# Expert layer as seven products of block sums for two token tiles

## The chip, the cores and the metric

The kernel runs on one core of one Trainium2 chip. Its engines are TensorE (PE, with its weight loads listed apart as PEld), VectorE (DVE), ScalarE (ACT), GpSimd (POOL) and SyncE (SP), which here issues the DMAs. They run side by side and wait for each other through semaphores. The metric is the time of the program on the device in microseconds; the kernel before takes 1626.39 us, the median of 3 runs (1625.09 to 1628.73).

## The reference

Four layers are applied to 1024 tokens of width 512 (16 x 64), each an attention and a feed-forward part added to the stream. The part that is changed is the third feed-forward, a layer of 64 experts of rank 16, in which every token takes its best 16 experts:

```
scores = xf @ Wr.T
top_vals, top_idx = jax.lax.top_k(scores, TOPK)
gates = jax.nn.softmax(top_vals, axis=-1)
G = jnp.zeros((N, K), xf.dtype).at[jnp.arange(N)[:, None], top_idx].set(gates)
h = jnp.einsum('nd,krd->nkr', xf, A)
out = jnp.einsum('nkr,kdr->nd', h * G[:, :, None], B)
return (out * SCALING).reshape(*prefix, -1)
```

All experts are computed for all tokens: a dense product of (tokens x 512) by (512 x 1024), a multiplication by the gates (zero for the experts not taken), and a product by (1024 x 512). Everything is in 32-bit floating point.

## The kernel before, in words

The tokens are 8 tiles of 128. Two lanes share the core, each with four of the eight PSUM banks and its own pools in SBUF: lane a allocates from the left, lane b from the right. Each lane is written as a generator that yields a cost in microseconds after each piece of work. `merged` runs lane a as the main one, and after each yield advances lane b by pieces whose costs add up to the same (times a rate). PE's order is this written order. The order of the other engines and of SP's queue is chosen by the framework's planner from the dependences and its own costs; each queue is then run in order.

Lane b does the first layer, then the second feed-forward (`mxfp4_ffn`) and the last layers for the first four tiles; lane a does the second layer's attention (`normed_attention`) for all eight tiles, then the same rest for the last four tiles. So lane b's `mxfp4_ffn` (about 750 to 850 us) and most of its expert layer (1039 to 1134 us) lie beside lane a's attention, the end of the latter beside lane a's `mxfp4_ffn`, and lane a's expert layer (1291 to 1412 us) lies beside lane b's last attention, `packed_attention`. From about 1450 us lane a is alone.

`mxfp4_ffn` quantises four tiles of weights (lane b only) and four of tokens by long chains of DVE instructions (L979 to L1004), turns them on PE (ps_mx) and multiplies. `small_head_attention` precedes the expert layer in each lane; its weights take three of the lane's pages, which are four buffers of 128 x 2048 f32 used in turn.

`lora_experts` loads four pages of weights (L1242), normalises and transposes the lane's tiles (`Normed`), and then runs four steps over the tiles, one behind the other: `router` (scores, the best 16, the gates), `hidden` (two PSUM banks of 512 columns, four products each, L1290, then a DVE multiplication by the gates, L1298), `turn` (eight transposes and two ACT copies, L1308) and, a tile later, `output` (eight products of 512 columns in one bank, L1315, and one DVE addition to the stream, L1318). A 128x512 f32 product appears in the trace as two records of PE. `packed_attention` follows; it starts by normalising the lane's first tiles and multiplying by the value weights (ps_v, L1411).

Of the kernel before, what the change touches and what calls it, by code (L numbers as in the profile page):

```python
# [8 lines left out]
F32 = mybir.dt.float32  # L9
F16 = mybir.dt.float16  # L10
F32R = mybir.dt.float32r
BF16 = mybir.dt.bfloat16
# [6 lines left out]
P = 128  # L19
# [27 lines left out]

PAGE = 2048


# [1000 lines left out]

def small_head_attention(ln, tiles, w_in):

# [14 lines left out]
    with ExitStack() as es:  # L1068
# [141 lines left out]

        for n in range(NTL + 3):
            if 0 <= n - 2 < NTL:
                values(n - 2)
                yield 1.0
# [15 lines left out]

def lora_experts(ln, tiles, w_a, w_r, w_b):


    k, nc = ln.k, ln.nc
    KE, R = 64, 16
    KR = KE * R
    SCALING = 2.0
    wa, wb = [], []
    for ws, src in ((wa, w_a), (wb, w_b)):
        for i in range(2):  # L1240
            ws.append(ln.page("w_l2f", PAGE))
            nc.sync.dma_start(ws[i], src[:, i * PAGE : (i + 1) * PAGE])  # L1242
    wa = [w[:, c * KR : (c + 1) * KR] for w in wa for c in range(2)]
    wb = [w[:, j * D : (j + 1) * D] for w in wb for j in range(4)]
    with ExitStack() as es:
        pool = ln.pool(es, "l2f")
        wr = w_r.rearrange("p (c n) -> p c n", c=NC)
        normed = Normed(ln, pool, tiles)
        normed.begin()
        yield 2.5  # L1250
        normed.need(-1)
        kept = {}

        def router(t):
            normed.need(tiles.index(t))
            ps = ln.bank([P, KE], "ps_r")
# [9 lines left out]
            for i in range(2):  # L1266
# [5 lines left out]
                best.append(m8)  # L1272
            gate = pool.tile([P, KE], F32, tag="gate", name="gate")
            nc.vector.tensor_tensor(gate, left, sc, ALU.not_equal)
# [6 lines left out]
            nc.vector.tensor_scalar_mul(gate, gate, sm[:, 1:2])  # L1281
            kept[t] = gate

        def hidden(t):
            gate = kept[t]
            hg = pool.tile([P, KE, R], F32, tag="hg", name="hg")
            for i in range(2):
                ps = ln.bank([P, KE // 2, R], "ps_h")
                for c in range(NC):
                    nc.tensor.matmul(  # L1290
                        ps,
                        lhsT=k.stream(c, t),
                        rhs=wa[c][:, i * 512 : (i + 1) * 512],
                        start=c == 0,
                        stop=c == NC - 1,
                    )
                part = slice(i * KE // 2, (i + 1) * KE // 2)
                nc.vector.tensor_tensor(  # L1298
                    hg[:, part, :], ps, bc(gate[:, part], 2, R), ALU.mult
                )  # L1300
            kept[t] = hg

        def turn(t):
            flat = kept[t].rearrange("p k r -> p (k r)")
            hT = pool.tile([P, KR // P, P], F32, tag="hT", name="hT")
            for i in range(2):
                ps = ln.transposed(flat[:, i * 512 : (i + 1) * 512], 4, "ps_hT")
                nc.scalar.copy(hT[:, 4 * i : 4 * i + 4, :], ps)  # L1308
            kept[t] = hT

        def output(t):
            hT = kept.pop(t)
            ps = ln.bank([P, D], "ps_o")
            for j in range(KR // P):
                nc.tensor.matmul(  # L1315
                    ps, lhsT=hT[:, j, :], rhs=wb[j], start=j == 0, stop=j == KR // P - 1
                )
            nc.vector.scalar_tensor_tensor(k.x[t], ps, SCALING, k.x[t], ALU.mult, ALU.add)  # L1318

        yield from ticks(  # L1320
            tiles,
            [(0, router, 0.9), (2, output, 6.9), (0, hidden, 6.9), (1, turn, 0.9)],
        )

# [282 lines left out]
def decoder_kernel(ctx: ExitStack, tc: tile.TileContext, i: dict, out: bass.AP):  # L1607
# [4 lines left out]
    halves = [list(range(NT // 2)), list(range(NT // 2, NT))]  # L1612
    kept_w = ctx.enter_context(
        tc.tile_pool(name="kept_w", bufs=1, space=bass.MemoryType.DRAM)
    ).tile([P, NC, D], BF16, tag="wT", name="wT_d")

# [45 lines left out]
    def last_layers(ln, tiles):  # L1662
        yield from small_head_attention(ln, tiles, i["l2a_w"])
        yield from lora_experts(ln, tiles, i["l2f_a"], routers[0], i["l2f_b"])
        yield from packed_attention(
            ln, tiles, i["l3a_w"], i["l3a_v"], [i["l3f_q"], i["l3f_r"], i["l3f_b"], out]
        )

    def side():
        yield from first_layers(b)  # L1670
        b.pages(ctx)

        routers.append(b.pool(ctx, "wr", 1).tile([P, NC * 64], F32, tag="wr", name="wr"))
        nc.sync.dma_start(routers[0], i["l2f_r"])
        yield from mxfp4_ffn(b, halves[0], i["l1f_w"], i["l1f_b"], kept_w)
        yield MARK
        yield from last_layers(b, halves[0])
# [18 lines left out]
def laid_out(a):  # L1696
# [52 lines left out]
    i["l2a_w"] = np.concatenate([chunks(m) for m in w], 1)  # L1749
    i["l2f_a"] = chunks(a["L2_ffn_A"].reshape(-1, D).T)  # L1750
    i["l2f_r"] = chunks(a["L2_ffn_Wr"].T)
    i["l2f_b"] = chunks(a["L2_ffn_B"].transpose(0, 2, 1).reshape(-1, D))
    w = [a[f"L3_xattn_W{n}"].T for n in "qkvo"]
# [26 lines left out]
```

## Time and profile before

| what | value |
|---|---|
| median of 3 runs | 1626.39 us |
| the profiled execution, its own time | 1626.99 us |
| its span, from the first to the last instruction | 1625.0 us |
| mean granted TensorE clock | 0.994 |
| busy: PE, DVE, ACT, POOL | 1571.1, 966.7, 618.2, 513.1 us |
| hidden products, L1290 | 128 records, 56.4 us |
| output products, L1315 | 128 records, 56.7 us |
| gate multiplications on DVE, L1298 | 16 of 0.69 us |
| output additions on DVE, L1318 | 8 of 0.69 us |
| loads of expert weights | 8 of 1024 KB, 5.0 to 5.2 us to landing |
| DMA moved | 200.32 MB |

A row of a group gives line, engine, operation, what is written and read, shapes, and count; then busy time and the mean duration of one in ns; then the engine's idle time just before, and what ended it. Busy time is the union of the instructions on an engine: PE's records overlap, so that the time from one start to the next is shorter than one's duration. In a timeline each row is a start, a length, the engine, the line and the instruction, with a count where several are merged, and in brackets the idle time before it. In the chain that ended last each step is followed back to what released it.

### The profile page before, as it was taken

The page shows a single profiled execution, that of the slowest core. Times are in us where ns is not written, and L with a number is a line of the kernel's source. Part 1 is how long each engine was busy: PE and PEld are TensorE (multiplying, and loading weights), DVE is VectorE, ACT ScalarE, POOL GpSimd, SP SyncE. Part 2 cuts the span into 40 slices and gives each one's busy share as a digit, 9 for nine tenths or more (in the row PEclk, how much of TensorE's full clock was granted, in tenths as well). Part 3 has the DMA queues.
Part 4 walks back from the last instruction along what each step waited for, and adds up shares of the span by engine and source line. Part 5 has one row for each costly group of instructions (what it writes and reads, how often), then busy time and mean ns, then how long its engine had stood idle before and what let it go on. Part 6 is the DMA issues. An engine that isn't in the chain of part 4 may idle for free.

```text
span 1625.0 us, 20864 instructions
## 1 busy us (share of the span) xinstructions
PE 1571.1 (97%) x7099; PEld 911.6 (56%) x7104; DVE 966.7 (59%) x2000; ACT 618.2 (38%) x1932; POOL 513.1 (32%) x526
## 2 busy tenths in 40 slices
PE   7899899999999999999999999999999999999999
PEld 2234456565565655666566565554566566557774
DVE  6687488676787577778944464447156333422335
ACT  3333444334443444444443353311245232224442
POOL 2394237631384314843321232111023001011112
PEclk9999899999999999999999999999999999999999
DMA  8892349623693436935442231032120102201120
GB/s 233 267 287 90 109 143 272 197 88 129 188 281 115 140 120 196 278 132 198 153 145 97 101 117 57 32 128 80 42 73 20 46 20 70 76 33 39 40 72 26
DMA packets 98472, 200.32 MB, mean 123 GB/s; under 512 B 48960, under 2 KB 66112, under 8 KB 86720
## 3 DMA queue, kind: packets, MB, share of 16 engines
q1 hardware_dynamic: 98368, 199.00, 39.0%
q8 instruction: 57, 0.93, 0.2%
q14 instruction: 47, 0.39, 0.1%
HBM read 179.57 MB, written 19.40 MB: 122 GB/s over the span
## 4 chain that ended last, share of the span: by engine, by line
PE 78%; DVE 11%; ACT 3%; DMA 3%; POOL 2%; issue 2%; SPq 0%; ACTq 0%; DVEq 0%; POOLq 0%
PE ps_wo L745 15%; PE ps_q L859 10%; PE ps_kv L877 5%; PE ps_q L1464 5%; PE ps_ckv L811 5%; PE ps_s L695 4%; PE ps_a L736 4%; PE ps_o L1315 3%; PE ps_h L1290 3%; PE ps_pT L142 3%; PE ps_v L1411 3%; DMA att<-att_d 2%; PE ps_k L1448 2%; PE ps_wo L1205 2%; PE ps_q L1137 2%
## 5 line engine op out<-in xcount | busy, mean ns | idle before, releaser
L745 PE MATMUL ps_wo<-l1a_o,aT 128*128 128x512 f32 x512 | 231.7, 595 | 3.1 <-ACT aT L929 3.1
L859 PE MATMUL ps_q<-l1a_w,kvT 128*128 128x512 f32 x512 | 233.5, 599 | 0.0
L711 ACT ACTIVATE p<-ps_s,mx 128x128 f32<-128x128 f32 x384 | 135.7, 370 | 209.1 <-DVE mx L706 192.5
L720 POOL TENSOR_TENSOR p<-p,sm 128x512 f32<-128x512 f32 x96 | 103.9, 1082 | 335.8 <-DVE sm L719 298.4
L124 POOL TENSOR_TENSOR r<-r,mhalf 128x5 f32<-128x5 f32 (+1 forms) x96 | 102.0, 1063 | 268.8 <-DVE r L801 265.5
L859 PEld LDWEIGHTS ps_q<-l1a_w,kvT 128*128 128x128 f32 x512 | 96.5, 192 | 117.1 <-issue 115.6
L745 PEld LDWEIGHTS ps_wo<-l1a_o,aT 128*128 128x128 f32 x512 | 93.0, 191 | 100.8 <-issue 96.2
L158 DVE TENSOR_TENSOR x<-x,ps_wo 128x512 f32<-128x512 f32 x104 | 70.6, 679 | 115.5 <-PE ps_wo L745 83.1
L877 PE MATMUL ps_kv<-l1a_w,kvT 128*128 128x256 f32 x512 | 122.2, 381 | 1.3 <-DVE x L158 1.2
L477 POOL TENSOR_TENSOR acc<-acc,pv 128x512 f32<-128x512 f32 x96 | 121.6, 1291 | 2.6 <-DVE pv L467 1.9
L811 PE MATMUL ps_ckv<-l1a_kv,kvT 128*64 128x512 f32 x512 | 116.9, 598 | 4.5 <-ACT ckv L820 4.5
L124 POOL TENSOR_TENSOR rs<-rs,mhalf 128x1 f32<-128x1 f32 x64 | 36.8, 580 | 254.4 <-DVE rs L133 222.8
L800 DVE TENSOR_REDUCE r<-sq 128x5 f32<-128x640 f32 x64 | 52.3, 817 | 106.3 <-ACT sq L885 106.3
L877 PEld LDWEIGHTS ps_kv<-l1a_w,kvT 128*128 128x128 f32 x512 | 92.5, 190 | 16.4 <-issue 3.0
L867 ACT ACTIVATE sq<-ps_q 128x512 f32<-128x512 f32 x64 | 38.3, 598 | 154.0 <-PE ps_q L859 154.0
L467 DVE TENSOR_TENSOR pv<-att,ps_v 128x512 f32<-128x512 f32 x128 | 82.2, 677 | 19.7 <-DMA att<-att_d 16.1
L695 PE MATMUL ps_s<-kT,qT 128*128 128x128 f32 (+1 forms) x704 | 92.1, 276 | 0.1
L370 DVE TENSOR_TENSOR prod<-qs,kp 128x1024 f32<-128x1024 f32 x64 | 80.9, 1301 | 14.9 <-ACT qs L351 7.5
L727 DVE COPY pT<-ps_pT 128x512 f32<-128x512 f32 x96 | 64.2, 682 | 39.5 <-PE ps_pT L142 39.4
L695 PEld LDWEIGHTS ps_s<-kT,qT 128*128 128x128 f32 (+1 forms) x704 | 85.0, 192 | 3.4 <-issue 2.1
L1464 PE MATMUL ps_q<-kvT,l3a_w 128*128 128x256 f32 x384 | 85.6, 379 | 0.0
L745 PE MATMUL ps_wo<-l3a_o,aP 128*128 128x512 f32 x192 | 85.5, 593 | 0.0
(195 smaller groups left out, 2716.2 us busy)
## 6 DMA issues: line engine op xcount, KB each, us to landing
l1a_w<-in_l1a_w SPq DMA_DIRECT2D x32, 1536.0 KB, 6.8
att<-att_d SPq DMA_DIRECT2D x64, 512.0 KB, 9.1
l1a_o<-in_l1a_w SPq DMA_DIRECT2D x32, 1024.0 KB, 5.1
s<-ckv SPq DMA_DIRECT2D x32, 256.0 KB, 5.0
l3a_w<-in_l3a_w SPq DMA_DIRECT2D x6, 1024.0 KB, 5.2
l3a_o<-in_l3a_w SPq DMA_DIRECT2D x8, 768.0 KB, 4.2
l1a_kv<-in_l1a_kv SPq DMA_DIRECT2D x4, 1024.0 KB, 7.7
dots_d<-dots SPq DMA_DIRECT2D x16, 256.0 KB, 2.4
```

The source lines that it names most:

```text
L124: self.nc.gpsimd.tensor_tensor(out, v, self.k.mhalf[:, : v.shape[1]], ALU.pow)
L370: nc.vector.tensor_tensor(prod, bc(qs, 1, 2), spaced(kp, b * NB + j + 2 * w, [[2, 2], [1, D]]), ALU.mult,)
L467: nc.vector.tensor_tensor(pv.rearrange("p (q w n) -> p q w n", w=2, n=L), att[:, a, :].rearrange("p (q w n) -> p q w n", w=2, n=L), spaced ...
L477: nc.gpsimd.tensor_tensor(sums, before, pv, ALU.add)
L695: nc.tensor.matmul(ps[:, i, :], lhsT=qT[:, i // 2, 2 * (i % 2) : 2 * (i % 2) + 2, :].rearrange("p g s -> p (g s)"), rhs=kTs[i // 2], start ...
L711: nc.scalar.activation(p[:, i, :], ps[:, i, :], AF.Exp, bias=mx[:, i : i + 1], scale=self.scale, accum_out=sm[:, i : i + 1],)
L720: nc.gpsimd.tensor_tensor(p, p, bc(sm, 2, P), ALU.mult)
L745: self.nc.tensor.matmul(ps, lhsT=a, rhs=wo[:, g, :], start=g == 0, stop=g == len(chunks) - 1)
L811: nc.tensor.matmul(ps[j * S : (j + 1) * S], lhsT=k.context(c, 2 * t + 1 - j), rhs=w_pair[hp][:, c, :], start=c == 0, stop=c == NC - 1,)
L859: nc.tensor.matmul(ps, lhsT=k.stream(c, t), rhs=w_qkv[n][0][:, c, :], start=c == 0, stop=c == NC - 1,)
L877: nc.tensor.matmul(ps, lhsT=k.stream(c, t), rhs=w_qkv[n][1][:, c, :], start=c == 0, stop=c == NC - 1,)
L1464: nc.tensor.matmul(ps[:, j], lhsT=wq[:, c, (j0 + j) * P : (j0 + j + 1) * P], rhs=k.kvT[:, c, t : t + 2, 1:3, :], start=c == 0, stop=c == N ...
```

## The change

Two tiles of tokens are taken as one matrix of two rows of blocks (the tiles) by two columns of blocks (halves of the inner dimension), and the weights as two by two blocks (halves of the inner dimension by halves of 512 columns). The product is then formed from seven block products instead of eight, in the form of Winograd: four sums of blocks on each side, seven products, seven additions of results. For the hidden layer this is done for each 512 of its 1024 columns; for the output once per pair of tiles.

The weights come in eight parts; each holds the blocks in three of the seven slots needed, and four sums. `block_sums` makes the sums of the weights once, on POOL, in steps between the yields of lane b's `mxfp4_ffn`, and stores them in DRAM (`kept_s`); it takes one page. Each lane then loads each part by two DMAs, one from the input and one from the stored sums: parts 0 to 2 inside `small_head_attention` (`ahead.load`), 3 to 5 at the start of `lora_experts` (4 and 5 into new tiles of its own pool), 6 and 7 after hidden(1,0). The sums of the stream (`stream_sums`) and of the turned hidden values (`hidden_sums`) are made on POOL, four operations per pair of tiles each, in buffers that exist once ("s", "sh"). The gates are now applied on POOL, after the result has been put together by DVE. The four steps over tiles are replaced by a written order over two pairs of tiles.

```diff
+def block_sums(ln, src, kept):
+    nc = ln.nc
+    n_parts = src.shape[0]
+    raw = ln.page("sums", PAGE)
+    sums = raw[:, PAGE // 2 :].rearrange("p (i n) -> p i n", i=4)
+    b11, b21, b22, b12 = (raw[:, i * W2 : (i + 1) * W2] for i in range(4))
+    nc.sync.dma_start(raw[:, : PAGE // 2], src[0])
+    yield
+    for n in range(n_parts):
+        nc.gpsimd.tensor_tensor(sums[:, 0], b12, b11, ALU.subtract)
+        nc.gpsimd.tensor_tensor(sums[:, 2], b22, b12, ALU.subtract)
+        yield
+        nc.gpsimd.tensor_tensor(sums[:, 1], b22, sums[:, 0], ALU.subtract)
+        nc.gpsimd.tensor_tensor(sums[:, 3], b21, sums[:, 1], ALU.subtract)
+        yield
+        nc.sync.dma_start(kept[n], raw[:, PAGE // 2 :])
+        if n + 1 < n_parts:
+            nc.sync.dma_start(raw[:, : PAGE // 2], src[n + 1])
+        yield
+
+class Seven:
+    LHS = ("a11", "s2", "a12", "s3", "s1", "a22", "s4")
+    RHS = (0, 4, 1, 5, 3, 6, 2)
...
+    def products(self, n):
+        out = []
+        for i in range(n):
+            if i % 2 == 0:
+                ps = self.ln.bank([P, 2, W2], self.name)
+            a, b = self.lhs[self.LHS[self.n]], self.RHS[self.n]
+            for e, w in enumerate(self.rhs):
+                self.ln.nc.tensor.matmul(
+                    ps[:, i % 2],
+                    lhsT=a(e),
+                    rhs=w[:, b * W2 : (b + 1) * W2],
+                    start=e == 0,
+                    stop=e == len(self.rhs) - 1,
+                )
+            out.append(ps[:, i % 2])
+            self.n += 1
+        return out
...
+class LoraWeights:
...
+    def load(self, n, room=None):
+        if n in self.parts:
+            return
+        w = self.ln.page("w_l2f", 7 * W2) if room is None else room
+        half = 3 * W2
+        self.ln.nc.sync.dma_start(w[:, :half], self.src[n, :, :half])
+        self.ln.nc.sync.dma_start(w[:, half:], self.kept[n])
+        self.parts[n] = w
...
-def lora_experts(ln, tiles, w_a, w_r, w_b):
+def lora_experts(ln, tiles, weights, w_r):
+    pairs = [tiles[0:2], tiles[2:4]]
...
+        for n in range(4):
+            weights.load(n)
+        for n in range(4, 6):
+            weights.load(n, pool.tile([P, 7 * W2], F32, tag=f"w{n}", name="w_l2f", bufs=1))
...
+        def stream_sums(p):
+            t, u = pairs[p]
+            blocks = [k.kvT[:, c : c + 2, v, 1:3, :] for v in (t, u) for c in (0, 2)]
+            a11, a12, a21, a22 = blocks
+            s = pool.tile([P, 4, 2, 2, S], F32, tag="s", name="sx", bufs=1)
+            nc.gpsimd.tensor_tensor(s[:, 0], a21, a22, ALU.add)
+            nc.gpsimd.tensor_tensor(s[:, 1], s[:, 0], a11, ALU.subtract)
+            nc.gpsimd.tensor_tensor(s[:, 2], a11, a21, ALU.subtract)
+            nc.gpsimd.tensor_tensor(s[:, 3], a12, s[:, 1], ALU.subtract)
...
+        def hidden(p, i):
...
+            def gated(v, j):
+                g = gates[v][:, (2 * i + j) * W2 // R : (2 * i + j + 1) * W2 // R]
+                nc.gpsimd.tensor_tensor(hg[v][:, j], hg[v][:, j], bc(g, 2, R), ALU.mult)
...
+            p1, p6 = m.products(2)
+            nc.scalar.copy(s[:, 0], p1)
+            add(s[:, 1], s[:, 0], p6)
+            yield 1.7
+            p2, p7 = m.products(2)
+            add(flat[t][:, 0], s[:, 0], p2)
+            gated(t, 0)
+            add(s[:, 0], s[:, 1], p7)
+            yield 1.7
+            p5, p4 = m.products(2)
+            add(flat[u][:, 1], s[:, 0], p5)
+            gated(u, 1)
+            add(s[:, 1], s[:, 1], p5)
+            add(flat[u][:, 0], s[:, 0], p4)
+            gated(u, 0)
+            yield 1.7
+            (p3,) = m.products(1)
+            add(flat[t][:, 1], s[:, 1], p3)
+            gated(t, 1)
+            yield 0.9
...
+        def hidden_sums(p):
+            t, u = (hTs[v] for v in pairs[p])
+            a11, a12, a21, a22 = t[:, 0:4], t[:, 4:8], u[:, 0:4], u[:, 4:8]
+            s = pool.tile([P, 3, 4, P], F32, tag="sh", name="sh", bufs=1)
+            nc.gpsimd.tensor_tensor(s[:, 1], a11, a21, ALU.subtract)
+            nc.gpsimd.tensor_tensor(a21, a21, a22, ALU.add)
+            nc.gpsimd.tensor_tensor(s[:, 0], a21, a11, ALU.subtract)
+            nc.gpsimd.tensor_tensor(s[:, 2], a12, s[:, 0], ALU.subtract)
...
+        def output(p):
+            x = [k.x[v].rearrange("p (j n) -> p j n", j=2) for v in pairs[p]]
+            def add(v, j, src):
+                nc.vector.scalar_tensor_tensor(
+                    x[v][:, j], src, SCALING, x[v][:, j], ALU.mult, ALU.add
                 )
...
+            p1, p6 = m.products(2)
+            nc.scalar.copy(s[:, 0], p1)
+            nc.vector.tensor_tensor(s[:, 1], s[:, 0], p6, ALU.add)
+            add(0, 0, s[:, 0])
+            yield 3.45
+            p2, p7 = m.products(2)
+            add(0, 0, p2)
+            nc.vector.tensor_tensor(s[:, 0], s[:, 1], p7, ALU.add)
+            yield 3.45
+            p5, p4 = m.products(2)
+            nc.vector.tensor_tensor(s[:, 1], s[:, 1], p5, ALU.add)
+            add(1, 1, p5)
+            add(1, 0, p4)
+            add(0, 1, s[:, 1])
+            add(1, 1, s[:, 0])
+            add(1, 0, s[:, 0])
+            yield 3.45
+            (p3,) = m.products(1)
+            add(0, 1, p3)
+            yield 1.7
...
-        yield from ticks(
-            tiles,
-            [(0, router, 0.9), (2, output, 6.9), (0, hidden, 6.9), (1, turn, 0.9)],
-        )
+        router(0)
+        yield 0.9
+        router(1)
+        yield 0.9
+        stream_sums(0)
+        router(2)
+        yield 0.9
+        yield from hidden(0, 0)
+        router(3)
+        yield 0.9
+        yield from hidden(0, 1)
+        stream_sums(1)
+        yield from turn(0, 0)
+        yield from hidden(1, 0)
+        for n in range(6, 8):
+            weights.load(n)
+        yield from turn(0, 1)
+        hidden_sums(0)
+        yield from hidden(1, 1)
+        yield from turn(1, 0)
+        out = output(0)
+        yield next(out)
+        yield from turn(1, 1)
+        hidden_sums(1)
+        yield from out
+        yield from output(1)
...
-        yield from mxfp4_ffn(b, halves[0], i["l1f_w"], i["l1f_b"], kept_w)
+        sums = block_sums(b, i["l2f_w"], kept_s)
+        for cost in mxfp4_ffn(b, halves[0], i["l1f_w"], i["l1f_b"], kept_w):
+            next(sums, None)
+            yield cost
+        for _ in sums:
+            pass
```

## The prediction

> **What bounds the kernel now.** I read the page first, its busy times and the shares of the chain that ended last.
>
> ```profile
> PE 1571.1 (97%) x7099; PEld 911.6 (56%) x7104; DVE 966.7 (59%) x2000; ACT 618.2 (38%) x1932; POOL 513.1 (32%) x526
> ...
> PE 78%; DVE 11%; ACT 3%; DMA 3%; POOL 2%; issue 2%; SPq 0%; ACTq 0%; DVEq 0%; POOLq 0%
> ```
>
> TensorE is busy for 97% of the span and carries 78% of the chain, so PE time saved is worth its full length wherever nothing else ends later. Next, stretches: mxfp4_ffn of lane b (750 to 805, tail to 850), expert layer of lane b (1030 to 1140, the second part beside lane a's mxfp4_ffn), expert layer of lane a (1284 to 1414). Columns after the bounds: length, then busy us and instructions of each engine.
>
> ```profile
> 750.00:805.00 55.00, 53.97 (x225) 34.07 (x224) 54.04 (x138) 23.68 (x80) 20.32 (x19) 1.00 0.60 213
> 805.00:850.00 45.00, 44.89 (x185) 27.13 (x185) 26.22 (x58) 18.46 (x65) 10.99 (x12) 1.00 0.41 140
> 1030.00:1092.00 62.00, 60.25 (x221) 34.15 (x220) 24.53 (x74) 14.18 (x43) 5.19 (x7) 1.00 0.24 89
> 1092.00:1140.00 48.00, 45.13 (x148) 22.12 (x150) 38.14 (x97) 6.03 (x12) 10.33 (x11) 1.00 0.29 102
> 1284.00:1414.00 130.00, 129.42 (x486) 76.71 (x485) 53.70 (x137) 35.13 (x128) 10.53 (x12) 1.00 0.18 58
> ```
>
> In all of them PE is full, but from 750 to 805 DVE is full as well (54.04 of 55), and from 1092 to 1140 it has 9.9 us left. The chain in order of time shows which ends last in the first stretch:
>
> ```profile
> 796.38 0.60 DVE u L1002
> 796.98 0.73 DVE r L800
> 800.18 1.51 ACT p L711 x8
> 802.52 1.99 PE ps_kv L877 x8
> ```
>
> Up to 797 it runs through DVE's queue. A DVE delay there reaches the end almost whole.
>
> **Seven products for eight (removed).** A 512-wide f32 product is two records. The lines L1290 and L1315 have 128 each, 256 together. The new code has per pair of tiles 2 x 7 x 2 products for the hidden layer and 7 x 4 for the output, 56 products of 256 columns, so 224 over four pairs, 448 records. The pitch of a record is read from the timeline of PE:
>
> ```profile
> 1405.62 7.03 PE L1315 MATMUL ps_o<-w_l2f,hT 128*128 128x512 f32 x16
> 1345.81 5.34 PE L1464 MATMUL ps_q<-kvT,l3a_w 128*128 128x256 f32 x24
> 802.52 1.99 PE L877 MATMUL ps_kv<-l1a_w,kvT 128*128 128x256 f32 x8 [0.30 <-DVE x L158]
> ```
>
> 512 columns: (7.03 - 0.592) / 15 = 0.429 us. 256 columns: (5.34 - 0.379) / 23 = 0.2157 us; the weight load of 0.190 us still fits under it. Before 256 x 0.429 = 109.9 us, after 448 x 0.2157 = 96.6 us: **-13.2 us**, half of it in each lane. The worst 256-wide group shown, 1.99 us for 8, gives a pitch of 0.230, 103.0 us and -6.9; that chain began late, so I take 13.2 and keep 6.9. The number of transposes and of router products does not change.
>
> [...]
>
> **The weights' sums (added, lane b's mxfp4_ffn).** 8 parts x 4 POOL subtractions of 128x256. POOL with two full operands of 128x512 took 1.27 us (L477, L1022); tensor_scalar took 0.644 at 512 and 0.401 at 256 (L590), a fixed part of 0.158, so a 256-wide two-operand one is estimated at 0.158 + 1.11 / 2 = 0.71 us, all 32 at 22.8 us. POOL has room (20.32 of 55 busy): queued behind them are lane a's p (L720) and r (L124), late by one or two operations, 0.7 to 1.4 us, and read by PE about a tick later; the stored sums are read some 70 us later. The cost is DVE: where both run, they stretch each other.
>
> ```profile
> 776.54 1.67 POOL L1022 TENSOR_TENSOR x<-x,bf 128x512 f32<-128x512 f32 x1 [2.28 <-DVE xn L135]
> ...
> 777.65 1.11 DVE L999 SCALAR_TENSOR_TENSOR u<-m,w_l1f 128x512 f32<-128x512 f32 x1
> ...
> 778.17 1.49 POOL L720 TENSOR_TENSOR p<-p,sm 128x512 f32<-128x512 f32 x1
> ...
> 779.28 0.93 DVE L1000 SCALAR_TENSOR_TENSOR u<-m,u 128x512 f32<-128x512 f32 x1
> ```
>
> Undisturbed these take 1.27, 0.68, 1.04 and 0.68. From 776 to 793 three L1022 and two L720 (5.9 us undisturbed) cost DVE 0.43 + 0.25 + 0.57 (an L979) = 1.25 us, 21%. Side units come every 11.8 us of PE (one mx turn at 797.80, the next at 809.98 and 821.60), so some 17 of the 32 operations fall between 753 and 802: 12.1 us x 21% = **+2.6**. Ends: 0 (the operations land between DVE's) and 12.1 (each blocks DVE for its whole length). Past 805 DVE has 18.8 us free, so the rest costs nothing while that cover holds.
>
> [...]
>
> The sums' 8 stores and 8 loads go through SP, where a store waiting for POOL holds the kT and v loads of lane a (L851, L856). Those are used two to four ticks, 24 us and more, after issue and land in 3.9 us: nothing, unless the hold exceeds 20 us. Traffic grows by 8 MB for the sums and by 6.3 MB for the wider parts (7 blocks for 4 read 896 KB x 8 per lane, before 4 x 1024 KB), with DMA at 0.60 at most here: nothing.
>
> **Adds in the expert layer (added).** Per lane DVE loses 8 gating multiplies and 4 output adds (12 x 0.69 = 8.3 us) and gets 4 x 7 + 2 x 11 = 50 of 128x256, between 0.42 (L637) and 0.48 (L622, from PSUM), say 0.45: 22.5. ACT gets 6 copies of 0.42. POOL gets 8 stream sums (0.71), 16 gates (0.60, from L720's 1.04) and 8 hidden sums (1.27): 25.5 us. In lane a, DVE 53.7 + 14.2 and POOL 10.5 + 25.5 of 130 are far below PE: nothing. In lane b the part beside lane a's mxfp4_ffn is the tight one: of the 48 us DVE has 9.9 free. It loses one router (2.3), 4 gates and 3 adds (4.8), and gets hidden(1,1) and both outputs, 29 adds, 13.0: net 5.8. POOL there gets 8 x 1.27 + 4 x 0.60 = 12.6 us; in this stretch L1022's 5.08 us stretched four L979 by 2.49 us, 49%, so 6.2 more. 12.0 - 9.9 = **+2.1** (0 to 8.5 with full blocking).
>
> **New waits of PE, which runs in written order.**
> - hidden_sums(1) writes the single "sh" buffer, which output(0) reads until its seventh product. Then three POOL operations (3.8 us, with semaphores an estimated 4.1) precede the second product of output(1), and only p1 (8 records, 1.73 us) and what the other lane puts between cover it. All later PE work is queued behind. Uncovered 2.4 per lane; I take 2.0 for lane b, where lane a's 6.5 cost units let several side steps run in a row, and 0 for lane a: **+2.0** (0 to 4.8).
> - stream_sums(1) likewise waits for hidden(0,1): DVE add, gate and two sums, 2.7 us, against one transpose pair and p1, 1.7: **+0.5** (0 to 2).
> - packed_attention's first buffers probably lie where the expert pool's weight tiles, read to the end, were (both pools are allocated first in their lane at that point): two normalised tiles (0.55 each) can be late at the turn; before, the v products waited 0.66 and 1.0 there. **+1.0** (0 to 3).
> - Three routers now stand ahead of the first hidden product; each needs a turn and an ACT copy (0.59): **+0.3** (-0.5 to 1).
> - Gone: waits of 0.84 on hg and 0.28 on hT in lane b, since turns now stand well behind their gates. Late next is the POOL gate, with 6 us of products between: **-1.1** (-1.5 to 0).
> - Loads of parts 4 to 7 land in about 5.1 us (w_l2f) and have hidden products of 6 us and the other lane ahead: nothing; up to 5 per lane without that cover. Parts 0 to 2 are loaded earlier than the weights were, inside the attention before, into pages that are free by then: nothing.
>
> **Sum.** -13.2 + 2.6 + 2.1 + 2.0 + 0.5 + 1.0 + 0.3 - 1.1 = -5.8 us. The profiled execution took 1626.99 us (span 1625.0), 0.6 above the median 1626.39; 1621.2 on its scale, **1620.6** on the median's.
>
> **Rivals.**
> - *Everything new is hidden.* PE is full and each lane fills the other's gaps. -13.2 - 1.1 = -14.3: 1612.1. Against it: DVE's queue ends last around 753 to 797.
> - *The chains break.* Each pair of products is a new bank with new operands; if every one started late like L877's 1.99, the gain is 6.9 against the 8.5 of costs above less 1.1: +0.5, no change, 1626.9. For it: L877's eight waits on DVE; against: only 3.7 us over 512 records.
> - *DVE and POOL exclude each other (slower).* In the two stretches where DVE has nothing to spare each POOL operation holds DVE fully: 12.1 + 8.5 + 3.8 - 1.1 - 13.2 = +10.1, 1636.5. It decides from the share s where 12.1 s + (12.6 s - 4.1) + 2.7 = 13.2, s = 0.59; rows show 0.21 and 0.49.
> - *The change doesn't bring seven products* cannot be: the count is in the code.
>
> **How the numbers follow.** A difference under 0.2% (3.3 us) is about what a measurement of this kernel can't tell from none. The forecast case, 1615 to 1623, gets 0.43, all hidden 0.14, no change 0.20 (1623.1 to 1629.6: broken chains, or the forecast with the sh and entry waits at their upper ends, 1625.4), slower 0.23 (blocking, or late weights). Faster 0.57, same 0.20, slower 0.23. The range goes from all hidden, 1612, to just under the blocking case, 1634, leaving out about a tenth on each side. The forecast case's own range, 1615 to 1623, stands beside it because cases of both signs hold weight.
>
> **What the changed profile would show.** PE records of the products: 448, with about 0.2157 us pitch; otherwise the first term is wrong. POOL some 74 us above 513. DVE's two-input instructions between 750 and 805 longer by some 2.6 us in sum and PE idle more before L877 or L859; if by 8 or more, the blocking rival holds. A wait of PE on POOL before the second product of output(1). The prediction is wrong if PE idles between 750 and 850 by more than 6 us more than now, if parts come late from DMA, or if the pitch is above 0.23.

## The result, and the profile after it

The changed kernel took 1639.91 us (median of 6, 1638.27 to 1642.60) against 1627.13 us of the kernel before (6 runs beside it): 1.0080 times, 95% interval 1.0067 to 1.0093. The forecast was 1620.6, so the sign was wrong. The profiled execution took 1640.36 us, its span is 1638.3, 13.3 more than before. First the page of the changed kernel, its busy times and the shares of the chain that ended last:

```profile
PE 1568.9 (96%) x7291; PEld 951.3 (58%) x7296; DVE 1000.4 (61%) x2076; ACT 621.3 (38%) x1944; POOL 592.4 (36%) x622
...
PE 76%; DVE 11%; DMA 4%; POOL 3%; ACT 2%; issue 2%; SPq 1%; ACTq 0%; POOLq 0%; DVEq 0%
```

PE is busy 2.2 us less, not 13.2, although the span grew; DVE gained 33.7 us and POOL 79.3 (the forecast said 74). Averages say no more. To place the loss I took points of equal work: PE's groups stand in the same written order up to the expert layer and again behind it, so the start of one group can be compared. Two stretches matter: the sums' (lane b's mxfp4_ffn and its tail, between two starts of ps_q of lane a) and the expert layers' (from the first ps_xT of lane b's to the first ps_v behind lane a's). The windows of the kernel before for them (length, then busy us of PE, PEld, DVE, ACT, POOL, the granted clock):

```profile
750.04:846.51 96.47, 95.34 (x399) 59.72 (x400) 77.86 (x188) 42.14 (x144) 30.21 (x29) 1.00 0.50 176
...
1036.43:1416.78 380.35, 368.90 (x1717) 221.32 (x1718) 175.38 (x438) 117.87 (x355) 52.83 (x57) 1.00 0.17 60
```

and of the changed kernel for the same work:

```profile
754.33:861.12 106.79, 98.20 (x399) 60.85 (x400) 87.61 (x188) 42.03 (x144) 56.64 (x61) 0.98 0.67 236
...
1051.05:1430.05 379.00, 360.49 (x1909) 259.95 (x1909) 195.90 (x506) 121.92 (x367) 104.61 (x120) 0.99 0.21 73
```

So the loss has three places. The first 750 us, whose code and order are the same, took 4.3 us longer (750.04 to 754.33). The sums' stretch took 106.79 us instead of 96.47: **+10.3**, of which PE's idle time is 7.5 (1.13 to 8.59) and longer busy time 2.9. DVE's 188 instructions, the same as before, are 9.75 us longer. The expert layers, where 13.2 should have been won, took 379.00 instead of 380.35: **-1.35**. PE's busy time fell there by 8.41 only, and its idle time rose from 11.45 to 18.51 (+7.1).

The timeline of PE in the changed kernel shows what stands in those idle times, and what follows them:

```profile
814.67 1.08 PE L143 MATMUL ps_qT<-ident,qn 128*128 128x128 f32 x4 [3.89 <-DVE qn L901]
...
816.27 2.86 PE L878 MATMUL ps_kv<-l1a_w,kvT 128*128 128x256 f32 x8 [0.30 <-DVE x L159]
...
1115.93 0.66 PE L143 MATMUL ps_hT<-ident,hg 128*128 128x128 f32 x4 [1.96 <-DVE uh L1383]
1117.62 3.02 PE L1273 MATMUL ps_o<-w_l2f,hT 128*128 128x256 f32 x8 [1.03 <-DVE hg L1383]
...
1137.11 1.99 PE L1273 MATMUL ps_o<-w_l2f,sh 128*128 128x256 f32 x8 [2.57 <-POOL sh L1420]
...
1404.08 2.76 PE L1273 MATMUL ps_o<-w_l2f,sh 128*128 128x256 f32 x8 [2.43 <-POOL sh L1420]
...
1409.32 1.89 PE L1273 MATMUL ps_o<-w_l2f,hT 128*128 128x256 f32 x8
```

The last line is the price that the forecast had counted on: eight 256-wide records in 1.89 us, a pitch of 0.2157. Three of the groups just behind a wait took 2.76 to 3.02 instead. That is a lower granted clock, in the windows of the same trace:

```profile
1115.00:1118.40 3.40, 1.44 (x8) 1.12 (x9) 3.40 (x10) 0.59 (x1) 2.38 (x4) 1.00 0.99 411
1118.40:1121.80 3.40, 3.40 (x10) 2.69 (x9) 3.40 (x6) 0.00 (x0) 2.09 (x2) 0.51 1.02 429
1121.80:1125.20 3.40, 3.40 (x21) 3.07 (x20) 3.40 (x12) 1.45 (x3) 0.00 (x0) 0.99 0.98 402
```

PE was busy for 1.44 of 3.40 us, and for the next 3.4 us it got half its clock: 10 records where 21 went afterwards, 1.7 us lost. The changed kernel has three such pieces in the expert layers' stretch (at 1118, 1224 and 1405) and one at 814; the kernel before has none between 521 us and its end. The one at 1224 lies between the two expert layers, in lane b's attention, behind a wait of 1.97 us that the kernel before does not have there. Now the stretch closes: -13.2 (seven products) + 7.1 (idle) + 3 x 1.7 (half clock) = -1.0, measured -1.35.

In the sums' stretch the chain in order of time names the way from POOL to PE:

```profile
811.81 0.86 POOL sums L1248
812.67 1.14 POOL r L125
813.83 0.69 DVE qn L901
```

and the timelines of POOL and then of DVE show what had made both of them late:

```profile
771.87 1.17 POOL L1244 TENSOR_TENSOR sums<-sums 128x256 f32<-128x256 f32 x1
773.01 1.17 POOL L1245 TENSOR_TENSOR sums<-sums 128x256 f32<-128x256 f32 x1
774.14 1.17 POOL L1247 TENSOR_TENSOR sums<-sums 128x256 f32<-128x256 f32 x1
...
810.33 0.72 POOL L1245 TENSOR_TENSOR sums<-sums 128x256 f32<-128x256 f32 x1
...
771.23 1.23 DVE L1003 TENSOR_TENSOR u<-u,lim 128x512 f32<-128x512 f32 x1
772.38 1.21 DVE L1000 SCALAR_TENSOR_TENSOR u<-m,w_l1f 128x512 f32<-128x512 f32 x1
773.51 1.21 DVE L1005 TENSOR_TENSOR q<-u,lim 128x512 bf16<-128x512 f32 x1
774.65 1.21 DVE L1001 SCALAR_TENSOR_TENSOR u<-m,u 128x512 f32<-128x512 f32 x1
```

DVE's take 0.68 alone and POOL's 0.72 (as the last POOL row shows, later in the same trace). Here both take about 1.2, as if they ran in turns. The first of the four DVE rows is beside lane a's p on POOL and takes 1.24 without the sums too (e1, below); the other three take 0.68 there. So each POOL operation costs DVE some 0.54 us here, 75% of its length and not 21%.

### The profile page after: what moved, and what is told of

Read it like the earlier page. It is cut to its first block, busy times and chain, and to the rows that moved or that the text cites. A ratio compares the mean times of both kernels' runs of the same rounds, so it can differ in the third digit from the quotient of the medians.

```text
span 1638.3 us, 21522 instructions
## 1 busy us (share of the span) xinstructions
PE 1568.9 (96%) x7291; PEld 951.3 (58%) x7296; DVE 1000.4 (61%) x2076; ACT 621.3 (38%) x1944; POOL 592.4 (36%) x622
## 4 chain that ended last, share of the span: by engine, by line
PE 76%; DVE 11%; DMA 4%; POOL 3%; ACT 2%; issue 2%; SPq 1%; ACTq 0%; POOLq 0%; DVEq 0%
PE ps_wo L746 15%; PE ps_q L860 10%; PE ps_kv L878 5%; PE ps_q L1629 5%; PE ps_s L696 4%; PE ps_a L737 4%; PE ps_ckv L812 3%; DMA att<-att_d 3%; PE ps_o L1273 3%; PE ps_pT L143 3%; PE ps_k L1613 3%; PE ps_v L1576 3%; PE ps_h L1273 2%; PE ps_wo L1206 2%; PE ps_q L1138 2%
## 5 line engine op out<-in xcount | busy, mean ns | idle before, releaser
L746 PE MATMUL ps_wo<-l1a_o,aT 128*128 128x512 f32 x512 | 235.0, 602 | 3.1 <-ACT aT L930 3.1
```

The costliest lines, as they stand in the source:

```text
L746: self.nc.tensor.matmul(ps, lhsT=a, rhs=wo[:, g, :], start=g == 0, stop=g == len(chunks) - 1)
```

## The experiments

The theory: (A) the sums hold DVE, and keep lane a's r waiting in POOL's queue, exactly where DVE ends last; (B) the single "sh" buffer and a DVE late with lane b's results stop PE in the expert layers; (C) a wait of some 2 us is dearer than its length, since half a clock may follow; and the +4.3 us of the unchanged part is chance. Rivals: the sums' traffic, the forecast's price of 2.6 with the rest chance, and others named run by run. All times of a stretch below are differences to the first trace of the kernel before, at the same points of equal work; "half clock" is the time lost to half-clock pieces by the clock's record in the trace.

```
kernel                     0-750  750-861  861-1425   half clock in the last two
changed                     +4.3    +10.3      -1.3     1.7   5.1
changed again (e8)          +3.2    +11.1      -1.9     3.4   5.1
e1 no subtractions          +4.8      0.0      -1.5     0     5.1
e2 before + sums            -2.1    +12.0      +1.7     3.4   1.7
e3 sums written later       +3.9     +9.5      -0.6     3.4   6.8
e4 e3 + sh split            +5.3    +10.5     -10.5     3.4   1.7
e5 one input, 128x512       +2.1    +13.9      -1.4     3.4   5.1
e9 memset                   +5.8     +5.6      -1.4     0     5.1
e10 one input, 128x256      +2.4     +6.8      -1.3     1.7   5.1
e6 e4, sums pinned          +4.8      0.0      -7.0     0     5.1
e7 e6 + turn(1,1) later     +3.9      0.0     -10.1     0     1.7
e11 e7 + hidden_sums early  +4.5      0.0     -10.6     0     3.4
before again (e12)          +5.3      0.0       0.0     0     0
```

### The sums away, and the sums alone

In e1 the four `nc.gpsimd.tensor_tensor` of `block_sums` are gone and raw blocks are stored; in e2 the generator, its DRAM tiles and its steps beside `mxfp4_ffn` are added to the kernel before:

```diff
--- e1, in block_sums
-        nc.gpsimd.tensor_tensor(sums[:, 0], b12, b11, ALU.subtract)
...
-        nc.sync.dma_start(kept[n], raw[:, PAGE // 2 :])
+        nc.sync.dma_start(kept[n], half[n % 2])
--- e2, in side() of the kernel before
-        yield from mxfp4_ffn(b, halves[0], i["l1f_w"], i["l1f_b"], kept_w)
+        sums = block_sums(b, i["l2f_w"], kept_s)
+        for cost in mxfp4_ffn(b, halves[0], i["l1f_w"], i["l1f_b"], kept_w):
+            next(sums, None)
+            yield cost
```

> The changed kernel without the 32 POOL subtractions that make the weights' sums; their loads, their stores (of raw blocks in place of sums) and their steps stay, so the products in the expert layer read wrong sums: that part of the computation is left out. Theory (each subtraction holds DVE while DVE is what ends last): the time between 750 and 861 falls by the 10.3 us that the changed kernel lost there, total 1628 to 1631 us; PE's idle time between 753 and 820 falls from 8.5 to about 1 us, and no wait of 3.9 us on qn is left. Rival 1 (the sums' 8 loads and 8 stores on SP and the DMA engines do it): 1638 to 1641, the waits stay. Rival 2 (the forecast's price of 2.6 us was right and the rest is chance in the granted clock): 1636 to 1638.

> The kernel before plus the weights' sums alone, made in lane b's mxfp4_ffn exactly as in the changed kernel and stored, but read by nobody; the expert layer keeps its eight products. Theory (the subtractions hold DVE): +9 to +11 us against the kernel before, 1636 to 1638 us, with the wait on qn of some 3 to 4 us near 815. Rival 1 (the forecast's price): +2.6, 1629 to 1630. Rival 2 (the loss belongs to the changed kernel's other parts, such as the weight loads that follow): 0 to +1.

e1: 1630.15 us (12 runs), 0.9987 times before [0.9971, 1.0003]. The stretch from 750 to 861 takes exactly the time of before, with all loads and stores in place: the traffic is out. e2: 1638.40 (7 runs), 1.0044 [1.0023, 1.0064]; its stretch loses 12.0. So the subtractions alone make this loss, on either kernel, and the forecast's 2.6 falls.

The 147 DVE instructions that the kernel before runs between 753 and 815 can be matched one by one in every trace. Their durations add up to 9.2 us more in the changed kernel, 8.6 in its second trace, 8.5 in e2 and -0.01 in e1.

### What holds DVE: three replacements for the subtraction

Of each, the first of the four subtractions of a part is shown:

```diff
-        nc.gpsimd.tensor_tensor(sums[:, 0], b12, b11, ALU.subtract)
--- e5
+        nc.gpsimd.tensor_scalar_mul(pair[0], raw[:, 0 : 2 * W2], 1.0)
--- e10
+        nc.gpsimd.tensor_scalar_mul(sums[:, 0], b12, 1.0)
--- e9
+        nc.gpsimd.memset(raw[:, PAGE // 2 : PAGE // 2 + 3 * W2], 0.0)
```

> The changed kernel with each of the 32 subtractions of the weights' sums (two inputs, 128x256, 0.72 us alone) replaced by a POOL multiplication of one input by 1.0 over 128x512 (0.64 us alone by L591's form), at the same steps, with the same loads and stores: POOL's queue is as full as before, only the second input is gone. The sums are not computed, so the expert layer's products are of other numbers: that part is left out. Theory A (a POOL operation with two inputs holds DVE's two-input ones): the stretch from 750 to 861 loses at most 3 us instead of 10.3, about 6 us over the kernel before. Theory B (lane a's r waits behind the sums in POOL's queue, whatever they are): the 3.9 us wait on qn stays and the stretch loses 7 to 10 us, about 12 over the kernel before.

e5 took 1641.40 us (5 runs), 1.0068 [1.0038, 1.0097]: no better than the subtractions. It was not the comparison that I wanted, because a multiplication by a constant over 128x512 takes 1.48 us alone, not L591's 0.64; POOL was occupied twice as long. What it shows is the queue: r stood behind four of them and lane b's x, and DVE stood for it.

```profile
796.46 0.69 DVE L901 TENSOR_TENSOR qn<-qn,r 128x512 f32<-128x512 f32 x1 [3.85 <-POOL r L125]
```

That wait and one of 3.51 were zero before. Two fairer replacements followed:

> The run with one input again, but 128x256 wide, so that an operation takes about the 0.72 us of the subtraction (the wide one had taken 1.48, not 0.64, so it was no fair comparison). The sums are not computed. Theory A (two inputs on POOL are needed for the hold): the excess of the 147 DVE instructions falls below 4 us and the stretch from 750 to 861 loses under 5. Theory B (the hold goes by POOL's time, whatever it reads): excess 7 to 10, loss 9 to 12.

> The changed kernel with each of the 32 subtractions replaced by a POOL memset of 128x768 (about 0.74 us by the 0.95 us of the one of 128x1024), which reads nothing; loads, stores and steps stay, the sums are not computed. In the changed kernel the same 147 DVE instructions between 753 and 815 took 9.2 us longer than before (8.6 in its second trace). Theory A (the hold comes of POOL reading SBUF with a full operand): the excess falls below 3 us, the stretch from 750 to 861 loses 1 to 4 us. Theory B (any POOL operation of that length holds DVE): the excess stays at 7 to 10, the stretch loses 9 to 12. Theory C (what counts is POOL's queue in front of lane a's r): the excess falls, but the stretch still loses 7 or more, with waits of DVE on r.

Each has one run, of 1634.65 us (e10) and 1636.71 us (e9). The result is mixed for both, and the kind of DVE instruction sorts it. Excess of the 147 instructions in us, split into those with two tensors as inputs (tensor_tensor, scalar_tensor_tensor), the tensor_scalar forms (one tensor), and the rest, such as reductions and copies out of PSUM; then DVE's added idle time:

```
                     all   two tensors  one tensor  reductions, PSUM   idle
changed              9.2       4.3         4.9           0.0            1.2
changed again        8.6       3.7         4.9           0.0            1.8
e5  one input, 1.48  8.9       3.8         5.1           0.0            6.7
e10 one input, 0.85  5.1       2.4         2.7           0.0            3.1
e9  memset, 0.74     8.8       0.7         8.0           0.0            2.0
```

A second input on POOL is not needed: e10's excess is smaller but far from zero (its own theory A wanted under 4, B at least 7; it fell between). With memsets, which read nothing, the two-tensor instructions of DVE lose 0.7 us instead of 4.3, and the tensor_scalar ones 8.0 instead of 4.9. The timelines of POOL and DVE in e9 show it; compare the rows of the changed kernel above:

```profile
774.30 0.74 POOL L1243 MEMSET sums<- 128x768 f32 x1
775.11 0.74 POOL L1245 MEMSET sums<- 128x768 f32 x1
...
774.64 0.68 DVE L1005 TENSOR_TENSOR q<-u,lim 128x512 bf16<-128x512 f32 x1
775.24 0.68 DVE L1001 SCALAR_TENSOR_TENSOR u<-m,u 128x512 f32<-128x512 f32 x1
```

So what POOL reads goes with how long DVE's two-tensor instructions are held: 4.3 us in sum beside two inputs, 2.4 and 3.8 beside one, 0.7 beside none. For the tensor_scalar ones it does not (4.9; 2.7 and 5.1; 8.0), and the rest lost 0.0 beside any of them. What sets tensor_scalar apart no run here shows. Of e9's theories none fits whole: the excess is that of B, but the stretch lost 5.6 us and not 9 to 12, of which DVE's idle time explains 2.0 at most. So the hold by itself does not set the loss: DVE was held about as long in e9 as in the changed kernel (8.8 and 9.2 us), which lost 8.6 without its half clock. How the loss divides between the held DVE and the queue in front of r is not shown.

### Moving the sums

e3 took the steps of `block_sums` out of `mxfp4_ffn` into lane b's `small_head_attention`, and loaded the parts three rounds later; e6 also ties each pair of subtractions behind the last POOL instruction written before it.

```diff
--- e3
-        for cost in mxfp4_ffn(b, halves[0], i["l1f_w"], i["l1f_b"], kept_w):
-            next(sums, None)
-            yield cost
+        yield from mxfp4_ffn(b, halves[0], i["l1f_w"], i["l1f_b"], kept_w)
...
+        for cost in small_head_attention(ln, tiles, i["l2a_w"], weights, first):
+            if sums is not None:
+                next(sums, None)
+            yield cost
--- e6, besides
+        with ln.tc.issue_after(ln.last_of(mybir.EngineType.Pool)):
             nc.gpsimd.tensor_tensor(sums[:, 0], b12, b11, ALU.subtract)
```

> The changed kernel with the sums' steps moved behind lane b's mxfp4_ffn into lane b's small_head_attention (about 865 to 990), where DVE is busy 4 to 18 us of every 25; the weight parts are then loaded three rounds later. Theory (the price of a subtraction is set by whether DVE ends last where it runs): the 10.3 us go and nothing comes back, 1628 to 1631 us. Rival 1 (a held DVE delays the attention's chain just as much): 32 x 0.54 us = 17 us of DVE, of which half or more shows, 1637 to 1640. Rival 2 (the later weight loads come late): PE waits for w_l2f after 1051, 3 to 6 us of the gain lost, 1633 to 1636.

e3: 1638.45 us (8 runs), 1.0048 [1.0030, 1.0065]; nothing won, and neither theory nor rivals had the reason. The trace has it: the written place orders PE alone, and the planner put the sums where POOL seemed free.

```profile
765.15 1.31 POOL L1244 TENSOR_TENSOR sums<-sums 128x256 f32<-128x256 f32 x1
```

So e3 was no move of the sums at all, and the 9.5 us of 750 to 861 stayed.

> The run with the sums moved and "sh" split, and in addition each step of the sums is tied in POOL's order behind the last POOL instruction written before it, so that the planner cannot pull the sums forward to 765 as it did there: they now run at 865 to 990, where DVE is half idle. Theory (the sums cost what they hold of a DVE that ends last): the 10 us between 750 and 861 go, the stretch after them loses at most 2, total 5 to 9 us below the kernel before. Rival 1 (in the attention they hold DVE too, and lane a's chain there runs through qn and r as well): 4 to 10 us of it come back, 0 to +4 against the kernel before. Rival 2 (the loads of parts 0 to 2 now come too late): PE waits on w_l2f.

e6 (with the split of e4, below): 1624.34 us (12 runs), 0.9949 [0.9928, 0.9971]. The sums now run from 854.55 on:

```profile
854.55 0.73 POOL L1245 TENSOR_TENSOR sums<-sums 128x256 f32<-128x256 f32 x1
```

The stretch from 750 to 861 costs 0.0, and what follows it up to the expert layers costs 0.0 too: 32 subtractions for nothing, where 10.3 had been paid. PE waits nowhere for w_l2f. Both rivals fall.

### The single "sh" buffer

```diff
-            s = pool.tile([P, 3, 4, P], F32, tag="sh", name="sh", bufs=1)
+            s = [pool.tile([P, 4, P], F32, tag=f"sh{i}", name=f"sh{i}", bufs=1) for i in range(3)]
```

> The kernel with the sums moved (the run before this one) and, on top, the buffer "sh" as three tiles, so that hidden_sums of the second pair waits for the first pair's fourth product and not for its seventh. Theory (the single buffer costs a wait of 2.4 to 2.6 us in each lane, and after each some 2 us at half the granted clock): 7 to 9 us less than the run before this one, 1620 to 1623 us; no wait of PE on sh near 1125 and 1390. Rival 1 (only the waits go, the clock halves anyway at the next one): 4 to 5 less, 1624 to 1626. Rival 2 (the next operand in line, the sum a21 + a22 or the gate before it, is as late): 0 to 2 less.

e4: 1632.47 us (12 runs), 1.0004 [0.9989, 1.0019], 6 us below e3. Both waits on sh are gone, and the expert layers' stretch went from -0.6 (e3) to -10.5: 10.0 us, of which 5.0 are the two waits and 5.1 three half-clock pieces fewer (6.8 to 1.7 us). That fits the theory's 7 to 9 better than rival 1 (the clock halves at the next wait anyway), but one trace can't part them: e6 has the same split, and three pieces in that stretch again.

### The wait that was left in lane b

```diff
--- e7
         yield next(out)
+        yield next(out)
         yield from turn(1, 1)
--- e11, besides
-        yield from hidden(1, 0)
+        first = hidden(1, 0)
+        yield next(first)
+        yield from turn(0, 1)
+        hidden_sums(0)
+        yield from first
```

> The run before this one, and in both lanes turn(1,1) and hidden_sums of the second pair stand one step later, behind the fourth output product of the first pair instead of the second. Theory (PE's waits of 2.4 and 1.0 us for uh and hg in lane b come of two output products being too short a cover for the DVE adds and the POOL gate that hold each other there, and cost another 1.7 to 3.4 us of halved clock): 3 to 6 us below the run before this one. Rival (hidden_sums then comes too late for the second product of the second pair, since only three products cover it): a wait on sh0 or sh1 in its place, 0 to +3.

e7: 1621.40 us (6 runs), 0.9940 [0.9918, 0.9962]. Its theory fell all the same. The wait is still there:

```profile
1105.07 0.66 PE L143 MATMUL ps_hT<-ident,hg 128*128 128x128 f32 x4 [2.41 <-DVE uh L1385]
```

These are the transposes of turn(1,0), whose values had long been gated; by the releaser, a DVE instruction that reads products of hidden(1,1), they wait for a PSUM bank. Against e6 the stretch gained 3.1 us, and 3.4 of it is two half-clock pieces fewer behind waits that both kernels have. So e7's own edit is worth nothing that I can show.

> The run with turn(1,1) later, and in both lanes turn(0,1) and hidden_sums of the first pair now stand behind the first two products of hidden(1,0) instead of behind all seven. In lane b these four POOL operations (some 6 us) then fall before lane a's mxfp4_ffn begins near 1093, not into it. Theory (the remaining wait of PE of 2.4 us near 1105 is for a PSUM bank that DVE reads late, because the hidden sums and the gates hold DVE while it has lane a's quantising to do): the waits of 2.4 and 1.0 us shrink below 1.5 together, 2 to 4 us below the run with turn(1,1) later. Rival (DVE is late by lane a's quantising alone): the waits stay within 0.5 us, and nothing is gained.

e11: 1619.66 us (6 runs), 0.9929 [0.9911, 0.9946]. The timeline of PE:

```profile
1102.45 0.66 PE L143 MATMUL ps_hT<-ident,hg 128*128 128x128 f32 x4 [0.26 <-DVE uh L1385]
1104.14 1.99 PE L1275 MATMUL ps_o<-w_l2f,hT 128*128 128x256 f32 x8 [1.04 <-DVE hg L1385]
...
1135.62 1.97 PE L143 MATMUL ps_xT<-ident,xn 128*128 128x128 f32 x8 [1.71 <-DVE xn L136]
```

2.41 became 0.26, so the hidden sums were what held DVE there; the 1.0 on hg stayed, and a new wait of 1.71 for the next stage's norm, with a half-clock piece behind it, took most of the gain. The two waits did shrink below 1.5 together, but the run won 0.5 us by the trace, not 2 to 4. Of all kernels e11 has the lowest median, 0.71% below the kernel before on the same chip: with three edits of order and one of buffers the seven products do pay.

### The part that nobody touched

> The changed kernel itself once more, for its time on the same chip and a second trace. Theory (the +4.3 us of its first 750 us, whose code is the same as before, is chance: which waits of PE are followed by a stretch of half clock differs from run to run): the difference at 750 us lies anywhere between -3 and +5, and the loss of 10.3 between 750 and 861 comes again within 2. Rival (something in the program, such as its place in memory, makes the first 750 us slower): +4 again.

> The kernel before once more, for a second trace of it: in all traces of kernels with the new expert layer so far the first 750 us, whose code is the same, took 2.1 to 5.8 us longer than in the first trace of the kernel before, in the trace of the kernel before plus the sums 2.1 us less. Theory (which waits in the first 750 us are met by a stretch of half clock is chance, and the first trace of before was one of its quick ones): the first 750 us take 0 to 6 us longer than in the first trace, as in the others. Rival (something in the changed program costs 4 us there): within 1.5 us of the first trace or below it. From 750 to the end the two traces of before agree within 2 us under either.

e8: 1640.04 us (10 runs), 1.0059 [1.0039, 1.0080]. e12: 1632.40 us, one run; its trace takes 5.3 us longer than the first trace of before up to 750 us and then stays within 0.1 us of it to the end. So the +4.3 us of the changed kernel's first 750 us does not belong to the change: the first trace of before was one of its quick ones (its 26 and 24 runs that the experiments are compared with have medians of 1631.8 and 1631.3). All six of its first runs were quick, 1625.1 to 1628.8, so whether that is chance or something of that session is open. Half clock is not the whole reason either: e9's first 750 us took 5.8 us longer with the same 10.2 us lost to half clock as in the first trace of before. The change itself costs what comes after: +9.0 us by the first pair of traces (13.3 - 4.3), +9.2 by e8.

## Why the prediction was wrong, by its own steps

The forecast's sum was -5.8. Past 750 us the change measured +9.0. The steps:

- **Seven products, -13.2: right.** 448 records at 0.2157. In the expert layers PE's busy time fell by 8.4 with 5.1 us of half clock in it, so by 13.5 without. The rival "chains break" (-6.9) is out.
- **The weights' sums, +2.6: the step that failed.** Measured +10.3, or 8.6 without its half-clock piece. Two of its readings were wrong. One is the 21%: it came from a row where POOL had one or two operations together, and three back to back gave 75% a time. DVE's work with one input was held as well: tensor_scalar made half of the excess (4.9 of 9.2). The forecast's own rows said so: the L979 that it counted as stretched (0.57 of its 1.25 us, and 2.49 us beside L1022 in the next section) is a tensor_scalar with one input. Twenty subtractions, not 17, fell before 816; 9.2 us of their 14.4 is a share of 64%, above the 0.59 from which the forecast's own slower rival decides. The other is lane a's r: "late by one or two operations", it was late by more: DVE stood 1.14 us for it and PE 3.89. The upper end, 12.1, was the better value; it was set aside for a row of other circumstances.
- **DVE beside lane a's mxfp4_ffn, +2.1: right in kind and nearly in size.** In lane b PE waited 0.36 + 1.96 + 1.03 us around 1115 where before it had 0.84: +2.5. In e11, with the hidden sums moved away, a wait of 2.41 there became 0.26.
- **"sh", +2.0: half.** 2.57 in lane b, but 2.43 in lane a as well, where I had said 0: what lane b puts between did not cover it. +5.0.
- **stream_sums +0.5, entry +1.0, routers +0.3, removed waits -1.1: small, and no one of them matters.** No wait on sx exists; the v products behind the expert layers wait 1.0 in all, before 1.7; routers 1.8 against 1.1; the old waits on hT are gone, and the old one on hg came back as 1.03. Between the two layers, where the forecast had no term, the lanes interleave otherwise: a second wait of 1.97 on p came and some on pT went, +0.7.
- **Half clock: not a term at all.** 6.8 us, one piece in the sums' stretch and three in the expert layers' (one of them behind that second wait on p), none in the kernel before there. It is the largest part of the miss that no step had.

Put together: sums 8.6 instead of 2.6 (+6.0), waits 7.1 instead of 4.8 (+2.3), half clock 6.8 instead of 0, products -0.3: 14.8, and the forecast missed by 14.8 (-5.8 against +9.0). The rest of the median's distance, 1620.6 against 1639.9, is the first 750 us, to within 0.2.

Of the rivals, "DVE and POOL exclude each other" gave +10.1 and named the place of its first part, DVE held by the sums (12.1 for a full hold, measured 8.6). That its sum came near the +9.0 is luck: its 8.5 was 2.5, its 3.8 of waits held the 2.0 for sh that was 5.0, and half clock, which it did not have either, filled what was left. The list of what would make the prediction wrong held it too: PE idled 7.5 us more between 750 and 861, and the limit had been 6.

## What to carry to other kernels

Before putting work on an engine with room, ask which other engine it holds and whether that one has time to spare: the same 32 subtractions cost 10.3 us beside a full DVE (54.04 of 55 us busy in the kernel before) and 0.0 us a hundred microseconds later, where DVE is busy for 4 to 18 us of every 25. Moving the steps in the source did nothing for them; look in the trace where the planner ran them, and tie them down. And price a wait of PE by more than its length: from 860 to 1440 us in the traces here, 27 of 49 waits of 1.75 us and longer had a half-clock piece, and 9 of 128 between 0.6 and 1.25 us; a piece costs 1.7 us.

## What I had not expected of the hardware

The granted clock falls to half (0.50 in the trace's record of it) in pieces of 3.4 us or a multiple of it, and whether a wait of some 2 us is followed by one looks like a coin's toss. The wait of 1.97 us of ps_pT for DVE's p stands at the same place in all fourteen traces, once or twice; 12 of its 25 instances have a half-clock piece at or behind them. In the changed kernel, and then in its second trace:

```profile
1222.99 0.63 PE L143 MATMUL ps_pT<-ident,p 128*128 128x128 f32 x4 [1.97 <-DVE p L1170]
1223.46 5.29 PE L1613 MATMUL ps_k<-kvT,l3a_w 128*128 128x512 f32 x8
```

```profile
1223.82 0.63 PE L143 MATMUL ps_pT<-ident,p 128*128 128x128 f32 x4 [1.97 <-DVE p L1170]
1224.29 3.60 PE L1613 MATMUL ps_k<-kvT,l3a_w 128*128 128x512 f32 x8
```

The same eight records took 5.29 and 3.60 us. From 860 to 1440 us in all traces, waits of PE of 0.6 to 0.75 us had a piece in 1 of 71 cases, up to 1.25 in 8 of 57 (some of them beside a longer wait), 1.75 to 2.25 in 14 of 27 and longer ones in 13 of 22. The record says more than that: in each trace all pieces begin and end on one grid of 3.413 us, and what sorts the cases is how full PE was in one window of it. In the fourteen traces from 30 to 1600 us, of the windows at full clock in which PE was busy for less than 40%, all 60 had a half-clock piece next; from 40 to 50% 30 of 45, from 50 to 60% 7 of 70, and above 60% none of 6125. Where the whole wait on p fell into one window, 10 of 12 had a piece; where the grid cut it in two, 2 of 13. So most of the toss is where the wait falls on the grid. Counted from the span's start, the grid lies elsewhere in two traces: in the kernel before, pieces begin at 168.86, 325.87 and 517.02 us, 46 and 56 times 3.4133 us apart; in the changed kernel at 814.65, 1118.43, 1224.25 and 1405.15 us, 89, 31 and 53 times apart, but no whole number of times from those of before. What sets the grid no run shows. A window need not be wholly idle for a piece to follow, as the row with 1.44 us of work in 3.40 shows.
